# Q's result leaves a projection block through two half-row buffers and two stores, not through one buffer of the row pool

## The chip, the core and the metric

The kernel runs on one core of a Trainium2 chip. The metric is the device time of one launch in microseconds. Five engines work side by side, each on its own queue in order: TensorE (PE, with its weight loads shown as PEld), VectorE (DVE), ScalarE (ACT), GpSimd (POOL) and SyncE (SP). In this kernel DMAs are issued by SP and by POOL. An engine that meets an instruction whose input or buffer is not ready stands there with all that is queued behind it.

## What is computed

A transformer layer in float32 on x of shape (2, 2048, 1024), cut here to what matters:

```python
x = x + attn(layernorm(x))
x = x + ffn(layernorm(x))

def attn(x):                      # one head, D = 256
    q, k, v = split(x @ Wqkv + bqkv)
    a = softmax(q @ k.T / sqrt(256))
    return (a @ v) @ Wo + bo

def ffn(x):                       # HID 1024, INT 2048, LAT 512
    rw = sum of the top 2 of x @ gate_w
    shared = relu(x @ up_w) ** 2 @ down_w
    routed = ((x @ fc1_w) @ expert_w * rw) @ fc2_w
    return layernorm(shared + routed) * ln_gamma + ln_beta
```

## The kernel before, in words

Every float32 matrix product is made of three products of float32r parts (high times high, low times high, high times low), so each operand is split into a high and a low part first: ACT casts the high part, DVE subtracts it for the low one (`split`, L141).

**The stage around the change** is the projection of x to q, k and v, about the first 300 us. It runs over eight blocks of 512 rows, numbered here 0 to 7 by the order in which they run. For each block `qkv_block` (L427) does eight parts: four v tiles of 128 rows (`v_tile`, L437), then two chunks of q and two of k (`qk_chunk`, L461), of 512 columns each. Each part gathers its sum in a PSUM bank of the pool `psa`, which has four. DVE takes a v tile out of its bank (L456, L457) into half of a half-row tile; two v tiles share one such tile, which is split into high and low parts one part later. ACT takes q and k out of theirs (L472, L475). k and v of the first four blocks go to DRAM from their own pools (L486). q goes to DRAM for every block, since the attention stage reads it later: before the change both chunks are written to one tile of the row pool, `got["q"]`, and after the second chunk POOL issues one store of 512 KB, `q_d` (L481).

**Beside each part** a function `after` (L740) puts work for the next block into the order. After the v tiles j = 0 to 3 `NormBlock.step` (L306) normalises the next block's four rows of 128 x 1024. Two of the four have their moments taken by ACT (`Moments`, L255: L262 sums, L274 squares; each writes a throw-away tile `junk` from the half-row pool, L269), the two others by DVE (L179). ACT writes the normalised row (L286), DVE transposes 32 x 32 tiles of it into `xblk` (L214), POOL stores that (`xt_d`, L219) and fetches it back in another order (`xt`, L227). After the fourth v tile come the last `xt` fetch and, for blocks 0 to 5, the four loads of the rows of the block after next (`xrow`, L193 called from L762). After the second q chunk and the two k chunks the fetched tiles are split into the next block's operands (`xha`, `xla`, L143 and L144); the fourth is split after the next block's first v tile, ahead of the first moments.

**What sets the order.** Blocks 0 to 6 stand in a `manual_schedule` region: every engine's queue has the order of the program. Block 7 and the attention stage stand outside it and are ordered by a planner; the feed-forward stage is again in written order.

**The pools.** A tile gets its buffer when it is allocated in that order; when all buffers of the pool are taken, the first instruction that writes the new tile waits until the last user of an old one has ended, a DMA included. The row pool (L71) has nine buffers of 128 x 1024 float32 for the x rows, `xblk`, `xt` and, before the change, q. When q is allocated, four x rows and four `xt` tiles hold eight of the nine. The half-row pool (L72) has four buffers of 128 x 512 float32. In the projection stage it serves the bias of v (`bv`, L106, from the start to the last v tile), the v tiles (two tiles per block, one after the other) and `junk` (four per block).

Of the kernel before, what the change touches and what calls it, by code (L numbers as in the profile page):

```python
# [11 lines left out]
AF = mybir.ActivationFunctionType  # L12
# [7 lines left out]
W = 512  # L20
# [5 lines left out]
def kernel(  # L26
# [21 lines left out]
    nc = tc.nc  # L48
# [7 lines left out]
    NDC = D // P  # L56
# [30 lines left out]
    def row(name):  # L87
        return rp.tile([P, C], FP, tag="r", name=name)

    def half(name):  # L90
        return hp.tile([P, W], FP, tag="h", name=name)

    def bank(pool, name):
        return pool.tile([P, W], FP, tag="b", name=name)

    def f32(t):
        return t.bitcast(FP)
# [14 lines left out]
    q_d = [dram.tile([P, C], FP, name=f"q_d{i}") for i in range(NBLK)]  # L112
# [36 lines left out]
    def split_late(t, hi, lo):  # L149
        nc.scalar.copy(hi, t)  # L150
        late_ops.append(lambda: nc.vector.tensor_tensor(lo, t, f32(hi), ALU.subtract))  # L151

    def flush():
        for f in late_ops:
            f()
        late_ops.clear()
# [11 lines left out]
    def cols(w, i, n):  # L168

        return w.rearrange("(c p) i -> p c i", p=P)[:, :, ts(i, n)]  # L170
# [168 lines left out]
    def x_chunk(xT, c, sl=slice(0, W)):  # L339
        return tuple(v.rearrange("p (c n) -> p c n", n=W)[:, c % 4, sl] for v in xT[c // 4])  # L340

    def piece(pr, c, n, sl):
        return tuple(v.rearrange("p (c n) -> p c n", n=n)[:, c, sl] for v in pr)
# [79 lines left out]
    def hl(t):  # L423

        return t.rearrange("p (s n) -> p s n", s=2)

    def qkv_block(n, wqkv, xT, parts, after):  # L427

        keep = n < BPB
        units = {a: (unit if n == BPB - 1 else ex_unit)(f"{a}{n}") for a in "kv"}
        if keep:
            kv[n] = [units["k"], units["v"]]
        got = {}

        def v_tile(t):  # L437
            pm = bank(psa, "pv")
            if t % 2 == 0:
                got["v"] = half("v")  # L440

            for c in range(NCC):
                xh, xl = x_chunk(xT, c, ts(t, P))
                w = wqkv[2][c // 4].rearrange("p (c n) -> p c n", n=2 * D)[:, c % 4]
                ops = [(pm, xh, w), (pm[:, :D], xl, w[:, :D])]
                for i, (o, x_, w_) in enumerate(ops[:: -1 if c % 2 else 1]):
                    nc.tensor.matmul(  # L447
                        o,
                        lhsT=x_,
                        rhs=w_,  # L450
                        start=c + i == 0,
                        stop=c == NCC - 1 and i == 1,
                        skip_group_check=True,
                    )
            vt = got["v"][:, ts(t % 2, D)]
            nc.vector.tensor_tensor(vt, pm[:, :D], bv_sb, ALU.add)  # L456
            nc.vector.tensor_tensor(vt, pm[:, D : 2 * D], vt, ALU.add)  # L457
            flush()
            split_late(vt, *(hl(units["v"])[:, s, ts(t, D)] for s in range(2)))

        def qk_chunk(a, dc):  # L461
            i = "qk".index(a)
            pm = bank(psa, "pq")
            acc = Pass3(pm, NCC)
            for c in range(NCC):
                acc.add(piece(wqkv[i], c, D, ts(dc, P)), x_chunk(xT, c))
            bias = bqk_sb[:, i * NDC + dc : i * NDC + dc + 1]
            flush()
            if a == "q":
                if dc == 0:  # L470
                    got["q"] = row("q")
                nc.scalar.activation(got["q"][:, ts(dc, W)], pm, AF.Identity, bias=bias)  # L472
            else:
                h, l = (hl(units[a])[:, s, ts(dc, W)] for s in range(2))
                nc.scalar.activation(h, pm, AF.Identity, bias=bias)  # L475
                nc.vector.scalar_tensor_tensor(l, pm, bias, f32(h), ALU.add, ALU.subtract)

        for j, (a, i) in enumerate(parts):
            v_tile(i) if a == "v" else qk_chunk(a, i)
            if (a, i) == ("q", NDC - 1):  # L480
                nc.gpsimd.dma_start(out=q_d[n], in_=got["q"])  # L481
            after(j)
        flush()
        if not keep:
            for a, d in (("k", k_d), ("v", v_d)):
                nc.gpsimd.dma_start(out=d[n], in_=f32(units[a]))  # L486
# [247 lines left out]
    def a_block(i, norm, xT, x3):  # L734
# [5 lines left out]
        def after(j):  # L740
# [23 lines left out]
            elif j > NB:  # L764
                split_tile(norm.x[j - NB - 1], j - NB - 1, nxt[0])

        qkv_block(order[i], wqkv, xT, V + QK, after)
        if nxt:
            return (after_next or [None])[0], nxt[0], lambda: split_tile(norm.x[3], 3, nxt[0])

    wqkv, xT = {}, new_xT("a")
    with tc.manual_schedule():
# [3 lines left out]
        for i in range(NBLK - 1):  # L776
            norm, xT, x3 = a_block(i, norm, xT, x3)
            if i == 1:
                for h in range(C // W):
                    nc.gpsimd.dma_start(  # L780
                        out=cols(fc2e, h, W), in_=fold[h].rearrange("p (c n) -> p c n", n=W)
# [371 lines left out]
    with tc.manual_schedule():  # L1153
        for b in range(NBB):
# [73 lines left out]
            for m, (p, i) in enumerate(UPS[b]):  # L1228
# [63 lines left out]
                elif m >= 2 * NK and p != "p7":  # L1292
                    n = {"p4": "p6", "p6": "p5", "p5": "p3", "p3": "p7"}[p]
# [46 lines left out]
            for j, p in enumerate(("p1", "p2", "p6", "p5", "p3", "p7", "p4")):  # L1340
# [12 lines left out]
                for k in range(NK - late):  # L1353
# [4 lines left out]
                    if more:  # L1358
# [3 lines left out]
                        if j >= 5 and k % 2 and k < 2 * NB:  # L1362
                            n = "p1" if j == 5 else "p2"
# [18 lines left out]
                if late:  # L1382
                    last_w = [next_piece() for _ in range(late)]
                    both = unit("last")
                    while len(sp) < late:
                        i = len(sp) + len(sp_cast) - late + 2
# [78 lines left out]
```

## Time and profile before

| | |
|---|---|
| median of 3 runs | 2318.88 us (2317.77 to 2319.33) |
| the profiled execution's own time | 2317.74 us |
| its span, first to last instruction | 2315.8 us |
| granted TensorE clock | 0.999 |
| PE busy | 2301.2 us |
| ACT, L472, q out of PSUM | 16 instructions, 686 ns median |
| POOL, L481, q's store | 8 of 512 KB, 537 to 558 ns to issue, 3.3 to 10.5 us to landing |
| POOL, L193, loads of x rows | 24 of 512 KB, 540 ns median to issue |

The views of one profiled execution are shown. A line of a timeline has the start in us, the length in us, the engine, the line of the kernel, the operation, the tiles written and read, how many were merged, and in brackets how long the engine had stood idle before it and for whom. A line of the waits has the total wait, the number of waits and the longest. A line of the stretches has the length, the busy time of PE, PEld, DVE, ACT and POOL with the number of instructions, the granted clock, the share of the DMA engines that was busy, and GB/s. A line of DMA issues ends with the time from the issue to the landing.

### The profile page before, as it was taken

How to read it: one execution, taken by the hardware profiler on the slowest of the kernel's cores; microseconds unless marked ns; L12 is line 12 of the kernel's file. 1: busy time of each engine (PE TensorE's matmuls, PEld its weight loads, DVE VectorE, ACT ScalarE, POOL GpSimd, SP SyncE). 2: the span in 40 equal slices, each digit the busy share in tenths (PEclk: the TensorE clock that was granted, in tenths of full speed). 3: DMA queues.
4: the chain of work that ended last, by engine and by line, in shares of the span. 5: the costliest groups of instructions: out<-in, count | busy, mean ns of one | idle time of the engine just before them, and what ended most of it. 6: DMA issues, size and time to landing. Idle time of an engine off the chain costs nothing.

```text
span 2315.8 us, 28854 instructions
## 1 busy us (share of the span) xinstructions
PE 2301.2 (99%) x10332; PEld 1893.0 (82%) x10332; DVE 1567.1 (68%) x2458; ACT 1184.5 (51%) x1950; POOL 286.9 (12%) x434
## 2 busy tenths in 40 slices
PE   9999999999999999999999999999999999999998
PEld 7888888888888788888888888888888887888886
DVE  6666569888888575797665577765456667435656
ACT  6555455555544633766562474674045557214245
POOL 3222211011000111110110111110000011000000
PEclk9999999999999999999999999999999999999999
DMA  7878759899976677786787698686568579566684
GB/s 258 298 275 279 245 153 253 237 301 295 229 186 195 218 222 228 256 288 196 217 244 254 214 320 306 193 242 222 192 218 273 195 233 290 190 192 192 204 246 150
DMA packets 237023, 544.21 MB, mean 235 GB/s; under 512 B 18592, under 2 KB 105120, under 8 KB 234832
## 3 DMA queue, kind: packets, MB, share of 16 engines
q1 hardware_dynamic: 170448, 302.56, 39.6%
q0 software_dynamic: 66432, 239.81, 35.3%
q8 instruction: 82, 1.34, 0.2%
q14 instruction: 61, 0.50, 0.1%
HBM read 412.78 MB, written 180.37 MB: 256 GB/s over the span
## 4 chain that ended last, share of the span: by engine, by line
PE 89%; DVE 5%; DMA 2%; ACT 2%; issue 2%; POOL 0%; SPq 0%; DVEq 0%; ACTq 0%; POOLq 0%
PE pd L131 32%; PE pu L131 32%; PE ps L131 8%; PE po L131 8%; PE pw L131 4%; PE pq L131 3%; DVE xblk L214 1%; PE pg L990 1%; PE pv L447 1%; DMA xt_d<-xblk 1%; PE pf L131 1%; DVE xla L144 1%; DVE st L179 1%; DMA w<-wt_lead 0%; DVE v L457 0%
## 5 line engine op out<-in xcount | busy, mean ns | idle before, releaser
L131 PE MATMUL pd<-w,sp 128*128 128x512 f32 x3336 | 758.2, 389 | 0.6 <-DVE sp L1202 0.5
L131 PEld LDWEIGHTS pd<-w,sp 128*128 128x128 f32 x3336 | 625.9, 188 | 131.7 <-DVE sp L1202 1.9
L131 PE MATMUL pu<-xh,w 128*128 128x512 f32 x2240 | 690.6, 389 | 0.0
L131 PEld LDWEIGHTS pu<-xh,w 128*128 128x128 f32 x2240 | 420.4, 188 | 89.6 <-DVE w L941 0.5
L131 PE MATMUL pu<-xl,w 128*128 128x512 f32 x1120 | 436.0, 389 | 0.0
L131 PEld LDWEIGHTS pu<-xl,w 128*128 128x128 f32 x1120 | 210.3, 188 | 44.3 <-DVE xl L151 0.3
L1197 ACT CAST sp<-h 128x512 fp32r<-128x512 f32 x238 | 146.6, 618 | 155.9 <-PE pd L131 118.7
L934 ACT CAST w<-w 128x512 fp32r<-128x512 f32 x251 | 153.3, 616 | 138.6 <-DMA w<-wt 116.1
L941 DVE TENSOR_TENSOR w<-w 128x512 fp32r<-128x512 f32 x251 | 171.9, 687 | 75.4 <-ACT w L934 75.1
L1202 DVE TENSOR_TENSOR sp<-h,sp 128x512 fp32r<-128x512 f32 x238 | 163.1, 687 | 68.9 <-ACT sp L1197 68.7
L131 PE MATMUL po<-p,v 128*128 128x512 f32 x768 | 194.1, 391 | 0.0
L131 PE MATMUL ps<-q,k 128*128 128x512 f32 x768 | 192.5, 390 | 0.0
L131 PEld LDWEIGHTS ps<-q,k 128*128 128x128 f32 x768 | 143.7, 188 | 29.9 <-ACT max L630 0.2
L131 PEld LDWEIGHTS po<-p,v 128*128 128x128 f32 x768 | 143.2, 188 | 29.2
L1143 ACT ACTIVATE h<-h 128x1024 f32<-128x1024 f32 x48 | 50.8, 1057 | 220.4 <-DVE h L1260 158.5
L151 DVE TENSOR_TENSOR xl<-xt,xh 128x512 fp32r<-128x512 f32 x108 | 74.4, 689 | 128.1 <-ACT xh L150 125.6
L627 ACT COPY s<-ps 128x512 f32<-128x512 f32 x128 | 74.9, 586 | 142.0 <-PE ps L131 141.7
L214 DVE STREAM_TRANSPOSE xblk<-xrow 128x1024 f32<-128x1024 f32 x60 | 121.0, 2016 | 9.4 <-ACT xrow L286 9.2
L632 DVE TENSOR_TENSOR max<-ps,max 128x512 f32<-128x512 f32 x120 | 82.4, 686 | 33.2 <-ACT s L627 32.1
L944 POOL DMA_DIRECT2D w_p<-w x95 | 50.7, 534 | 405.8 <-DVE w L941 314.6
L131 PE MATMUL pq<-xha,w_h 128*128 128x512 f32 x256 | 99.8, 390 | 0.2 <-DVE v L457 0.2
L131 PE MATMUL pq<-xla,w_h 128*128 128x512 f32 x256 | 99.6, 389 | 0.0
(199 smaller groups left out, 2999.9 us busy)
## 6 DMA issues: line engine op xcount, KB each, us to landing
w<-w_p SPq DMA_DIRECT2D x230, 512.0 KB, 3.9
w<-wt SPq DMA_DIRECT2D x235, 256.0 KB, 3.4
w_p<-w POOLq DMA_DIRECT2D x95, 512.0 KB, 4.4
xt_d<-xblk POOLq DMA_DIRECT2D x56, 512.0 KB, 4.2
xt<-xt_d POOLq DMA_DIRECT2D x56, 512.0 KB, 5.8
xres<-in_L_attn_x_dram SPq DMA_DIRECT2D x32, 512.0 KB, 7.0
xres<-in_L_attn_bo_dram POOLq DMA_DIRECT2D x32, 512.0 KB, 10.3
x<-xres SPq DMA_DIRECT2D x32, 512.0 KB, 4.8
```

Of the source, the lines that this page charges most:

```text
L131: nc.tensor.matmul(self.ps, lhsT=a, rhs=b, start=self.i == 0, stop=self.i == self.n - 1, skip_group_check=self.on,)
L144: eng.tensor_tensor(lo, t, f32(hi), ALU.subtract)
L151: late_ops.append(lambda: nc.vector.tensor_tensor(lo, t, f32(hi), ALU.subtract))
L214: nc.vector.transpose(b.rearrange("p (q k i) -> p q k i", q=P // SQ, i=SQ), r.rearrange("p (k i q) -> p q k i", k=NCC, i=SQ),)
L627: nc.scalar.copy(s["s"][k // 4][:, ts(k % 4, W)], pm)
L632: nc.vector.tensor_tensor(s["max"], pm, s["max"], ALU.max)
L934: nc.scalar.copy(w[:, 0:W], raw)
L941: nc.vector.tensor_tensor(w[:, W : 2 * W], raw, f32(w)[:, 0:W], ALU.subtract)
L944: nc.gpsimd.dma_start(out=kept[key], in_=w.bitcast(FP))
L1143: nc.scalar.activation(o, v, AF.Relu)
L1197: nc.scalar.copy(t[:, 0:W], v)
L1202: add(t[:, W : 2 * W], v, f32(t)[:, 0:W], ALU.subtract)
```

## The change

Each chunk of q gets a half-row tile of its own and its own store of 256 KB, issued right after the chunk is taken out of PSUM. The row pool no longer serves q, and the single store after the second chunk is gone. The pools keep their sizes.

```diff
@@ in qk_chunk
             if a == "q":
-                if dc == 0:
-                    got["q"] = row("q")
-                nc.scalar.activation(got["q"][:, ts(dc, W)], pm, AF.Identity, bias=bias)
+                q = half("q")
+                nc.scalar.activation(q, pm, AF.Identity, bias=bias)
+                nc.gpsimd.dma_start(out=q_d[n][:, ts(dc, W)], in_=q)
             else:
@@ at the end of qkv_block
         for j, (a, i) in enumerate(parts):
             v_tile(i) if a == "v" else qk_chunk(a, i)
-            if (a, i) == ("q", NDC - 1):
-                nc.gpsimd.dma_start(out=q_d[n], in_=got["q"])
             after(j)
```

## The prediction

> **What bounds the kernel now.** I read the page's busy times first, then PE by stage, then who waits for whom between 64 and 270 us (blocks 1 to 6 of the projection stage), then the order of work on ACT, POOL, DVE and PE there, and last the transfers' times to landing.
>
> ```profile
> PE 2301.2 (99%) x10332; PEld 1893.0 (82%) x10332; DVE 1567.1 (68%) x2458; ACT 1184.5 (51%) x1950; POOL 286.9 (12%) x434
> ```
>
> TensorE leaves 14.6 us of a span of 2315.8 idle, so a change outside it can win at most that. In the stage that the change touches there is less: PE is busy for the whole of every stretch between 50 and 300 us but one.
>
> ```profile
> 180.00:220.00 40.00, 40.00 (x192) 33.34 (x191) 29.26 (x58) 23.98 (x43) 10.20 (x17) 1.00 0.76 265
> 220.00:260.00 40.00, 39.79 (x190) 32.91 (x190) 28.61 (x50) 22.80 (x40) 11.83 (x19) 1.00 0.84 281
> ```
>
> ```profile
> ACT q L472 <- DMA xt_d<-xblk: 41.1, 6, 7.0
> ...
> POOL xt L227 <- ACT q L472: 4.4, 1, 4.4
> ...
> PE pq L131 <- DVE v L457: 0.2, 1, 0.2
> ```
>
> The first line is the wait that the change aims at: in six blocks ACT stands before q's result for some 6.9 us, because q takes its buffer from the row pool and gets the one that the last transposed row still leaves through. The last line says what this costs PE today: 0.2 us.
>
> ACT around one block boundary (start, length, engine, line, operation):
>
> ```profile
> 97.19 1.27 ACT L472 ACTIVATE q<-pq,bqk_sb 128x512 f32<-128x512 f32 x2 [6.90 <-DMA xt_d<-xblk]
> ...
> 101.57 1.15 ACT L143 CAST xha<-xt 128x512 fp32r<-128x512 f32 x2
> 104.84 0.41 ACT L150 CAST v<-v 128x256 fp32r<-128x256 f32 x1 [2.12 <-DVE v L457]
> 105.15 1.14 ACT L143 CAST xha<-xt 128x512 fp32r<-128x512 f32 x2
> 106.19 1.05 ACT L262 ACTIVATE junk<-xrow 128x1024 bf16<-128x1024 f32 x1
> ```
>
> POOL before it, and how long its fourth row load and q's store took to land:
>
> ```profile
> 97.62 0.77 POOL L227 DMA_DIRECT2D xt<-xt_d  x1 [2.81 <-issue]
> 98.38 2.12 POOL L193 DMA_DIRECT2D xrow<-in_L_attn_x_dram  x4
> 100.49 0.54 POOL L481 DMA_DIRECT2D q_d<-q  x1
> ```
>
> ```profile
> xrow<-in_L_attn_x_dram POOLq DMA_DIRECT2D x1, 512.0 KB, 8.1
> q_d<-q POOLq DMA_DIRECT2D x1, 512.0 KB, 8.8
> ```
>
> q's store is queued behind four 512 KB loads: the fourth, issued at 99.97, lands at 108.1 and q's store at 109.3. The same store in the last block (290.58), with nothing ahead, lands after 3.3 us.
>
> DVE and PE after the boundary:
>
> ```profile
> 116.02 0.42 DVE L457 TENSOR_TENSOR v<-pv,v 128x256 f32<-128x256 f32 x1
> ```
>
> ```profile
> 249.68 0.47 PE L131 MATMUL pq<-xha,w_h 128*128 128x512 f32 x1 [0.21 <-DVE v L457]
> ```
>
> The second q chunk of a block uses the PSUM bank of that block's second v tile (pool psa has four), which L457 frees. It is freed 10.25 us after the block's first junk in each of blocks 1 to 6 (106.19 to 116.44), and the chunk starts soon after: 84.33, 117.23, 150.14, 183.16, 216.18 and 249.68, so the slack is 1.1, 0.8, 0.4, 0.15, 0.3 and 0. PE has almost no cover for a later junk.
>
> **The change, part by part.**
>
> *Removed: q's wait for a row buffer.* ACT can take q's first half at 89.9 in this block rather than at 97.19 (PE ended it at 84.3), and the second right behind. What is late next: the third split still waits for k's second chunk, which PE ends at 100.8, and the last two tiles' fetches (landed 99.4 and 101.8), and the v cast for PE's first v tile (103.4). So ACT would reach junk at about 105.8, not 106.19. PE can gain what it loses to this chain: its distances between blocks are 32.91, 32.90, 32.91, 33.14, 33.10 and 33.38, against 32.91 free, so 0.23 + 0.19 + 0.47 = 0.9 us over the stage.
>
> *Same work:* sixteen evictions of 0.69 us on ACT, none added. The row pool has one buffer more for x's rows; no row of the waits view but q's shows a wait for that pool, so nothing.
>
> *Added: eight DMA issues on POOL.* One of 0.54 us each, 4.3 us in all. They come behind the row loads; behind them are k_d, v_d and the weight sums of L409/L415, whose landing nobody in this stage waits for, and POOL is busy for 12% of the span. Nothing; without that cover 4.3 us. The later readers of q_d need both halves: the two at 265.1 read stores that landed by 242.3, and the load at 269.94 on SP (behind which stand the residual rows of the attention stage) reads block 6's, which then lands as one 512 KB store's worth as now. Nothing.
>
> *Added: a wait for a half-row buffer.* The pool `half` has four. One holds bv until the last v tile. Each block takes one for v tiles 0 and 1, four short ones for junk (L269), one for v tiles 2 and 3, and now two for q, held until q's stores land. When the next block begins, its first v pair takes the free one, bv and the two q halves hold the other three, and junk, allocated right after that v tile, finds none. It must take a q half and wait for its landing, as q did for xblk's. In the trace of before no junk waits, so the price comes from the landing rows.
>
> When does the first half land? POOL keeps the order of the program: xt, four loads, then q, whenever ACT was done (in block 6 q was ready at 257.8 and its store left at 264.51, behind the last xt at 263.76). So the half leaves at 100.49 in block 1, and at 67.11, 133.53, 168.37, 199.97 and 233.61 in the others. From there the fourth load lands after 8.6, 7.6, 8.4, 7.5, 8.9, 7.4 us (blocks 0 to 5; read from its row, less the 0.5 between the issues) and the whole q store after 9.9, 8.8, 9.6, 8.7, 10.5, 8.7. The first half carries half the bytes behind the same loads, so I take the middle: 9.2, 8.2, 9.0, 8.1, 9.7, 8.0, sum 52.2. Ends for the range: the fourth load (48.4), and the second half, which I put at the whole store plus 0.3 (58). Far below both lies the 3.3 of the lone store.
>
> junk stands 5.7 us behind the issue now (100.49 to 106.19). A landing after 8.2 makes it wait some 2.5. Queued behind it on ACT are the moments, the normalised rows, the v casts and q; DVE waits for those at L279 with the second v tile's eviction behind it; PE waits for that bank. And the delay adds up, since the chain closes on itself: from junk to the next q issue (normalise, transpose, xt_d, xt, four loads) the trace has 27.5, 27.3, 28.9, 27.2 and 28.0 us in blocks 1 to 5, with ACT and DVE nearly back to back and PE ahead of them. In block 3 the xt issue came 1.8 after its xt_d landed, not 0.5 (the 4.4 behind ACT q above); I drop that 1.3, leaving 137.6. Then the first junk of block 6 comes at 67.1 + 52.2 + 137.6 + six wake-ups of 0.1 (97.1 to 97.19 for q) = 257.5, against 239.28: 18.2 us late. One turn takes 27.5 + 8.7 + 0.1 = 36.3 where the blocks now follow each other in 33.3. In block 6 PE has no slack, so PE is 18.2 late there, and everything after runs at 99% PE and gives nothing back.
>
> The Trainium skill, "DMA: Bandwidth & Descriptors", section "Anatomy of one DMA — SWDGE (gpsimd) path", fits such a transfer as 2.0 us plus bytes over 436 GB/s: by estimate 2.6 us for a half and 3.2 for the whole, which the lone store's 3.3 agrees with and the 8.8 behind four loads does not. By that rule the half would land before junk is reached and the sum would be -0.9; by the rows it is +18.2, and I go by the rows, as the queue ahead is part of the landing. Its section "Bandwidth" asks for batches of 1 MiB and more, which speaks against halving a store.
>
> **Sum.** The profiled execution took 2317.74 (span 2315.8), so 2335.9; the median shown, 2318.88, is 1.1 above it: 2337.1. By the ends: 67.1 + 48.4 + 135.6 (0.4 less a turn for the xt lag) + 0.6 gives +12.4, 2331; 67.1 + 58 + 138.9 + 0.6 gives +25.3, 2344.
>
> **The rivals.**
> 1. *No junk waits* (ends on the other side). If a half lands within 5.7 us of its issue, the wait is gone and 0.9 us is won: 2318.0. The lone 3.3 speaks for it, the fourth load's 7.4 or more ahead in the same queue against it.
> 2. *The new v pair, not junk, gets a q half.* Then DVE's v eviction stands at the landing, and junk follows 2.3 later (103.93 to 106.19): 6 x 2.3 = 13.8 more, +32.0, 2351. Against it: the pair is allocated first, while one buffer is free.
> 3. *junk waits for the second half*: 2344, as above.
> 4. *The half lands in between*, at 6.5 us: 67.1 + 39 + 137.6 + 0.6 = 244.3, +5.0, 2324.
> 5. The last block and the attention stage are ordered by a planner, which may shift their order: some 2 us either way, inside the range.
>
> **How the numbers follow.** The main case 0.65, junk on the second half 0.10, the v pair 0.07, in between 0.06, no wait 0.12. The measurement tells 0.2%, 4.6 us. No wait is "same" but for 0.03 that something else wins more: faster 0.03, same 0.09, slower 0.88. The range 2323 to 2347 holds the main case, the second half and about half of "in between".
>
> **What would show it.** ACT q without a wait for xt_d; the four junk instructions (or v L456) of blocks 1 to 6 with waits for q_d of some 3 us each; PE idle of about 18 us at pq behind DVE v L457; the v tiles' starts 36 us apart; the stages after it unchanged but shifted. I am wrong if the half lands early, if POOL sends it ahead of the loads, or if a junk finds a free buffer.

## The result, and the profile after

The changed kernel takes 2329.72 us (median of 6 runs, 2328.98 to 2332.15) beside 2318.70 for the kernel before (6 runs, 2317.77 to 2320.36). The ratio is 1.0048, 95% interval 1.0038 to 1.0058: 11.0 us slower. The forecast was 18.2 us slower (2337.1), with a range of 2323 to 2347. The profiled execution of the changed kernel took 2329.25, its span 2327.4.

The page of the changed kernel, busy times:

```profile
PE 2304.1 (99%) x10332; PEld 1895.5 (81%) x10332; DVE 1568.1 (67%) x2458; ACT 1185.1 (51%) x1950; POOL 291.4 (13%) x442
```

The work is the same; PE's idle time went from 14.6 to 23.3 us, and its busy time from 2301.2 to 2304.1, 1.8 us of that in one chunk at a lower clock (last section). Who waits for whom between 60 and 310 us:

```profile
ACT junk L262 <- issue: 20.8, 6, 4.5
...
PE pq L131 <- DVE v L457: 8.4, 5, 2.4
```

The six waits of ACT before q (41.1 us) are gone. In their place stand six waits before the first `junk` of blocks 1 to 6, 20.8 us, and PE's wait for the second v tile's bank went from 0.2 to 8.4 us (the prediction's signs had some 18 there, and a wait before each of a block's four `junk`; only the first waits). The profile names no releaser for these waits ("issue"); the times do. ACT at the boundary that the prediction showed (block 1 to block 2), then POOL before it and the time to landing of the fourth load and of q's first half:

```profile
105.52 1.14 ACT L143 CAST xha<-xt 128x512 fp32r<-128x512 f32 x2
110.17 1.06 ACT L262 ACTIVATE junk<-xrow 128x1024 bf16<-128x1024 f32 x1 [3.51 <-issue]
...
111.46 0.28 ACT L183 ACTIVATE sd<-mv,eps 128x1 f32<-128x1 f32 x1
```

```profile
98.89 0.77 POOL L227 DMA_DIRECT2D xt<-xt_d  x1 [2.54 <-issue]
99.70 2.12 POOL L193 DMA_DIRECT2D xrow<-in_L_attn_x_dram  x4
101.82 1.09 POOL L472 DMA_DIRECT2D q_d<-q  x2
```

```profile
xrow<-in_L_attn_x_dram POOLq DMA_DIRECT2D x1, 512.0 KB, 8.1
q_d<-q POOLq DMA_DIRECT2D x1, 256.0 KB, 8.3
```

The first half leaves at 101.82, lands 8.3 us later at 110.1, and junk starts at 110.17. So it is in each of the six blocks (the store is that of the block before):

| block | first half issued | to landing | landed | junk in the changed kernel | junk before |
|---|---|---|---|---|---|
| 1 | 66.46 | 9.1 | 75.5 | 75.60 | 72.99 |
| 2 | 101.82 | 8.3 | 110.1 | 110.17 | 106.19 |
| 3 | 136.19 | 8.5 | 144.7 | 144.79 | 139.48 |
| 4 | 170.44 | 9.6 | 180.0 | 180.09 | 172.76 |
| 5 | 206.39 | 9.2 | 215.6 | 215.68 | 205.62 |
| 6 | 241.88 | 8.3 | 250.2 | 250.29 | 239.28 |

The delay of junk grows from 2.6 to 11.0 us. DVE and PE in block 2, where the second v tile's bank is freed and the second q chunk takes it:

```profile
118.89 0.42 DVE L457 TENSOR_TENSOR v<-pv,v 128x256 f32<-128x256 f32 x1
```

```profile
119.46 0.47 PE L131 MATMUL pq<-xha,w_h 128*128 128x512 f32 x1 [1.40 <-DVE v L457]
```

The second q chunk of block 6 starts at 259.60 and not at 249.68, 9.9 us late, and the stage's last chunk ends at 309.50 and not at 299.15, 10.3 us late. The span is 11.6 longer: what the stage lost stays lost, as the later stages keep PE full, and in the feed-forward stage of this execution PE waits 1.1 us more for DVE than in the one of before (1.6 and 0.5).

### The profile page after: what moved, and what is told of

Same layout as the page of the kernel before. It is cut to its first block, busy times and chain, and to the rows that moved or that the text cites. A ratio compares the mean times of both kernels' runs of the same rounds, so it can differ in the third digit from the quotient of the medians.

```text
span 2327.4 us, 28898 instructions
## 1 busy us (share of the span) xinstructions
PE 2304.1 (99%) x10332; PEld 1895.5 (81%) x10332; DVE 1568.1 (67%) x2458; ACT 1185.1 (51%) x1950; POOL 291.4 (13%) x442
## 4 chain that ended last, share of the span: by engine, by line
PE 86%; DMA 4%; DVE 3%; issue 3%; ACT 2%; POOL 1%; DVEq 0%; POOLq 0%; ACTq 0%; SPq 0%
PE pd L131 31%; PE pu L131 31%; PE ps L131 8%; PE po L131 7%; PE pw L131 4%; PE pq L131 2%; DVE xblk L214 1%; PE pg L988 1%; DMA q_d<-q 1%; PE pf L131 1%; DMA xt<-xt_d 1%; DMA xt_d<-xblk 1%; DMA w<-wt_lead 0%; ACT junk L274 0%; ACT junk L262 0%
## 5 line engine op out<-in xcount | busy, mean ns | idle before, releaser
L131 PE MATMUL pq<-xha,w_l 128*128 128x512 f32 x256 | 100.4, 392 | 0.0
```

The lines of the kernel that those rows point to most:

```text
L131: nc.tensor.matmul(self.ps, lhsT=a, rhs=b, start=self.i == 0, stop=self.i == self.n - 1, skip_group_check=self.on,)
```

## The experiments

All ratios are to runs of the kernel before on the same chip.

**1. junk without the half-row pool.** The moments' throw-away tile of the projection stage moves to the row pool, which has a buffer to spare since q left it.

```diff
         def junk(self):
-            return half("junk").bitcast(mybir.dt.bfloat16)
+            t = row("junk")[:, 0:W] if self.early else half("junk")
+            return t.bitcast(mybir.dt.bfloat16)
```

(Lines that pass `early` on are left out here; it is set by `NormBlock` alone.)

> The changed kernel, with the throw-away tile of the moments in the projection stage taken from the row pool, where a buffer is free since q left it, and not from the half-row pool. My theory (junk waits for a q half's landing, and that wait is the whole loss): ACT junk without a wait in blocks 1 to 6, PE idle before pq under 1 us, some 2318 us, 11 below the changed kernel and within 2 of the kernel before. Rival (the loss comes from the second store and the shorter rows themselves, or from the freed row buffer's new order): 2328 to 2331, as the changed kernel.

Measured: 2317.32 us, ratio 0.9995 (0.9986 to 1.0005). ACT and PE in this kernel:

```profile
104.23 1.14 ACT L143 CAST xha<-xt 128x512 fp32r<-128x512 f32 x2
105.27 1.05 ACT L262 ACTIVATE junk<-xrow 128x1024 bf16<-128x1024 f32 x1
```

```profile
220.00:260.00 40.00, 40.00 (x193) 33.61 (x192) 27.39 (x50) 22.57 (x40) 12.40 (x20) 1.00 0.83 281
```

junk starts with no wait, and PE waits for nothing in blocks 1 to 6. The q stores are as before the edit, two of 256 KB behind four loads, and land after 8.2 to 9.5 us; only nobody waits for them. So the whole loss hangs on junk's buffer. Run again in more rounds, with the question whether the two buffers win anything once junk does not wait:

> The kernel of junk_in_rows once more, in more rounds, to see whether the two half-row buffers win anything where junk does not wait. My working has 0.9 us to win (PE's distances between blocks back to 32.91), a ratio of 0.9996; the rival that q's wait cost more than PE's idle shows would give 0.998 or less. Where the interval spans 1, the trace alone tells of the 0.9.

Measured: 2318.30 us, ratio 0.9993 (0.9984 to 1.0002). The time does not tell it from the kernel before. In the first of its two profiles the blocks follow each other at 32.9 us throughout, and from the first q chunk to the end of the last k chunk the stage takes 252.3 us (45.34 to 297.62; 252.3 in the second profile too) beside 253.2 in the one profile of the kernel before (45.97 to 299.15): the 0.9 us of the prediction, and no more.

**2. The row loads behind q's stores.** The four loads are issued after the second q chunk, so that in POOL's queue the two halves stand ahead of them.

```diff
             if j == NB - 1:
                 norm.step(NB)
-                if i + 2 < NBLK:
-                    after_next.append(NormBlock(load_block(xf, order[i + 2], nc.gpsimd)))
                 nxt.append(new_xT(f"a{i}"))
             elif j > NB:
+                if j == NB + 1 and i + 2 < NBLK:
+                    after_next.append(NormBlock(load_block(xf, order[i + 2], nc.gpsimd)))
```

> The changed kernel, with the four row loads issued after the second q chunk and not after the fourth v tile, so that on POOL the two q stores stand ahead of them, still behind the last xt fetch. My theory (the four loads ahead in the queue make the landing late): a q half lands some 4 to 5 us after its issue, 1 to 2 us before junk is reached, no junk wait, some 2318 us. Rival (POOL's position does not matter, the bytes of the stage do): landing after 8 us or more, 2326 to 2330 us.

Measured: 2320.40 us, ratio 1.0003 (0.9994 to 1.0012). The times to landing of the q stores between 60 and 245 us, first in the changed kernel, then in this one:

```profile
DMA to landing us min/median/max: 8.3/8.8/9.7
```

```profile
DMA to landing us min/median/max: 4.6/4.8/5.8
```

The same stores land in 4.8 us rather than 8.8 when the loads stand behind them. junk then waits 2.0 us in all of the stage, none of it for q's store, and the loss is gone. In this kernel the landing is late because of what stands ahead in POOL's queue, and that is the written order.

**3. q's stores on SP.**

```diff
-                nc.gpsimd.dma_start(out=q_d[n][:, ts(dc, W)], in_=q)
+                nc.sync.dma_start(out=q_d[n][:, ts(dc, W)], in_=q)
```

> The changed kernel, with the sixteen q stores issued on SP and not on POOL, so that they do not stand behind the four row loads. My theory (the landing is late because of the queue ahead of it): a q half lands within 4 us of its issue and long before junk, junk without a wait, some 2318 us. Rival (a half-row store lands late in this stage whatever queue it is on, since the 16 DMA engines are full of the same bytes): landing after 6 to 8 us, but as the issue is some 8 us earlier the junk wait would still shrink to nothing or 1 us; then the two theories differ in the landing alone.

Measured: 2322.15 us, ratio 1.0011 (1.0002 to 1.0020). On this queue nothing stands ahead, and still the halves land after 5.3 to 7.5 us, not within my 4; the rival's 6 to 8 was nearer. But they leave some 9 us (block 0) to 16 us (block 5) earlier than in the changed kernel. junk waits once, for 1.2 us before 207.08, and not for q, which had landed at 197.72, but by the times for its x row (landed at 207.01). Most of the loss is gone. Some 2.6 us remain: PE stands for 1.4 us before second q chunks, and for 2.4 in block 7's v tiles, for splits of the fetched tiles. The q stores go at the time when the transposed tiles are stored and fetched back, and what waits longer in this kernel (between 100 and 310 us) is the split for its fetched tile and DVE's statistics for their row:

```profile
ACT xha L143 <- DMA xt<-xt_d: 18.7, 9, 8.0
...
DVE st L179 <- DMA xrow<-in_L_attn_x_dram: 5.1, 4, 1.7
```

In the kernel before, the first of these is 6.5 us in the same stretch and the second does not occur; the second is 4.0 us in experiment 2 as well, which loses nothing by it. That the stores took the other transfers' share of the DMA engines fits this, but was not tried by itself.

**4. Eight PSUM banks.** The parts of a block go over all eight banks, so that no q chunk needs a v tile's bank of its own block.

```diff
-            pm = bank(psa, "pv")
+            pm = bank((psa, psb, psc, psa)[t], "pv")
...
-            pm = bank(psa, "pq")
+            pm = bank(((psa, psb), (psc, psa))[i][dc], "pq")
```

> The changed kernel, with the v tiles and the q and k chunks spread over all eight PSUM banks (pools psa, psb and psc) and not over psa's four, so that a chunk of q no longer needs the bank of a v tile of its own block. My theory (the wait closes a chain on itself, junk to junk through the transposes, the fetch, the loads and the q store, and takes some 35 us per turn where PE needs 32.9): the junk waits stay, and PE is caught later, by the splits of the next block; 2 to 5 us won of the 11, some 2325 to 2328. Rival (PE only ever loses at the bank, block by block): 2318 to 2320.

Measured: 2332.30 us, ratio 1.0055 (1.0040 to 1.0070); the changed kernel's interval overlaps it. Nothing was won, so both expectations missed the number, the rival by far. Waits of the stage in this kernel:

```profile
ACT junk L262 <- DMA q_d<-q: 25.4, 4, 7.3
...
ACT junk L262 <- issue: 7.4, 2, 5.1
```

```profile
PE pv L447 <- ACT xha L143: 7.3, 6, 4.6
...
PE pv L447 <- DVE xla L144: 2.0, 7, 0.5
```

The profile names q's store as what junk waits for in four of the six blocks here. PE runs ahead through the free banks and is then caught by the splits of the next block, as my theory has it. What I put at 2 to 5 us did not come: the longest gap, 4.6 us, now comes in block 7, and the clock is at half when PE resumes. In these lines PE's busy time is the second number, and the granted clock stands behind the five engines (1.00, then 0.55, 0.50, 0.50):

```profile
280.00:282.00 2.00, 0.00 (x0) 0.00 (x0) 0.00 (x0) 0.00 (x0) 2.00 (x5) 1.00 0.90 348
282.00:284.00 2.00, 0.00 (x0) 0.00 (x0) 1.26 (x3) 1.91 (x4) 0.23 (x1) 0.55 1.06 363
284.00:286.00 2.00, 1.45 (x4) 0.94 (x5) 2.00 (x5) 0.84 (x2) 0.00 (x0) 0.50 0.98 354
286.00:288.00 2.00, 2.00 (x7) 1.69 (x7) 1.46 (x5) 0.41 (x1) 0.00 (x0) 0.50 1.03 418
```

By the trace some 3 us go to the clock: block 7's v tiles take 20.2 us, against 11.3 in the kernel before, and 5.9 of that are waits. Another 2.2 us are the chain, which is no shorter here but longer (junk of block 6 starts at 253.35, 3.1 later than in the changed kernel, in an execution that began 0.9 later). Why block 7's gap is so long, and what part the planner's order has in it, is left open.

**5. A fifth load ahead of the stores.**

```diff
                     after_next.append(NormBlock(load_block(xf, order[i + 2], nc.gpsimd)))
+                    load_row(xf[ds(order[i + 2] * W, P), :], nc.gpsimd)
```

> The changed kernel with a fifth row load of 512 KB (into a row buffer that nobody reads) behind the four, so ahead of q's stores, in blocks 0 to 5. My theory (junk waits for the first q half, and the wait is paid anew in each turn of the chain junk to q store to junk): the first half lands about 1.3 us later in each of six turns (0.5 of it for POOL's issue), junk comes six times 1.3 later, some 8 us on top: 2336 to 2340. Rival (the loss of each block is its own, with no chain): the same 1.3 once, 2330 to 2332.

Measured: 2339.78 us, ratio 1.0087 (1.0070 to 1.0104), 21.1 us above the kernel before, 10 more than the changed kernel. junk of block 6 starts at 260.64, 10.4 us later than in the changed kernel; 0.9 of that is the execution's later start (first q chunk at 46.30 and 45.41), so each of the six turns grew by 1.6. Paid once it would have been 1.6. In this execution (2342.40 us, the longest of the four) another 2.5 us are a chunk of block 6 at a lower clock (last section). The waits of the stage:

```profile
ACT junk L262 <- issue: 15.2, 3, 6.8
...
ACT junk L262 <- DMA q_d<-q: 13.8, 3, 5.4
```

**6. Half-row buffers in blocks 0 to 2 alone.**

```diff
             if a == "q":
-                q = half("q")
-                nc.scalar.activation(q, pm, AF.Identity, bias=bias)
-                nc.gpsimd.dma_start(out=q_d[n][:, ts(dc, W)], in_=q)
+                if order.index(n) < 3:
+                    q = half("q")
+                    nc.scalar.activation(q, pm, AF.Identity, bias=bias)
+                    nc.gpsimd.dma_start(out=q_d[n][:, ts(dc, W)], in_=q)
+                else:
+                    if dc == 0:
+                        got["q"] = row("q")
+                    nc.scalar.activation(got["q"][:, ts(dc, W)], pm, AF.Identity, bias=bias)
+                    if dc == NDC - 1:
+                        nc.gpsimd.dma_start(out=q_d[n], in_=got["q"])
```

> Q's two half-row tiles and stores in blocks 0 to 2 alone; blocks 3 to 7 as before the change (row buffer, one store). My theory: junk waits in blocks 1 to 3, is 5.3 us late in block 3 as in the changed kernel, and nothing after gives it back, since PE is full: before + 5, some 2324. Rival (the later blocks have slack and take the delay in): 2319 to 2321.

Measured: 2323.23 us, ratio 1.0018 (1.0009 to 1.0028), 4.5 us. junk is late by 6.5 us in block 3 (145.98) and, with no q half to wait for any more, still by 6.0 in block 6 (245.25); 0.4 of both is the execution's later start. The later blocks give back at most 0.5: the delay is kept.

**7. Two stores from one row buffer.** The kernel before, with each half of q's row buffer stored right after its eviction.

```diff
-                nc.scalar.activation(got["q"][:, ts(dc, W)], pm, AF.Identity, bias=bias)
+                q = got["q"][:, ts(dc, W)]
+                nc.scalar.activation(q, pm, AF.Identity, bias=bias)
+                nc.gpsimd.dma_start(out=q_d[n][:, ts(dc, W)], in_=q)
...
-            if (a, i) == ("q", NDC - 1):
-                nc.gpsimd.dma_start(out=q_d[n], in_=got["q"])
```

> The kernel before with the stores alone changed: q stays in one row buffer, but each half of it is stored by its own DMA, right after its eviction. My theory (a second store and shorter rows cost nothing by themselves): ACT q still waits 6.9 us for xt_d in six blocks, no junk waits, 2317 to 2320. Rival (the second store, its issue on POOL or its 2 KB rows cost time): 2321 or more.

Measured: 2317.53 us, ratio 0.9996 (0.9986 to 1.0005). The wait that the change removes is all there, and neither it nor the second store with its 2 KB rows adds anything that the time shows; the interval leaves room for 1.2 us. (The stage takes 254.6 us in this one profile, 253.2 in that of before.)

```profile
ACT q L473 <- DMA xt_d<-xblk: 42.7, 6, 7.8
```

## Why the prediction was right, and where its size was off

- **q's wait for a row buffer was worth 0.9 us.** Shown: experiment 7 keeps the wait and takes the time of before, experiment 1 has neither wait and wins 0.9 us by its traces. The times alone do not tell so little.
- **The issues on POOL cost nothing.** Shown by experiment 7 (eight issues more, and no loss over its interval's 1.2 us, where they would be 4.3 without cover). Nor does halving the store, which the prediction held against the change.
- **junk must wait for a q half.** Shown: the table's landings and starts agree within 0.1 us in six blocks, and experiment 1 takes the loss away by giving junk another buffer. It is the first half that it waits for: the second half of block 1's q lands at 110.7, after junk of block 2 has begun at 110.17. Rivals 1 to 4 fall with this and with landings after 8.3 us and more; the v pair stands where it did, its adds ending at 105.18 (104.8 before).
- **The landing behind four loads.** I had 52.2 us for the six landings, and 53.0 were measured, each 0.3 to 0.8 after the fourth load's. Experiment 2 shows that the loads ahead make it late (4.8 us without them). The 2.6 us that the prediction worked out from the Trainium skill ("DMA: Bandwidth & Descriptors", section "Anatomy of one DMA — SWDGE (gpsimd) path") leave the queue out; where nothing stands ahead, in block 7, a half lands after 2.2 to 2.3 us.
- **The chain that closes on itself.** Shown by experiment 5 (10 us more for 1.6 us more per turn), by experiment 6 (a delay that stays), and by the growth in the table: from junk to junk the turns take 34.9 us on average, where 36.3 were forecast and PE by itself needs 32.91. Experiment 4 shows that the bank is only where PE meets it.
- **The term that was mis-sized: the turn from junk to the next q issue.** I took its five values of before, 137.6 us; measured are 26.2, 26.0, 25.7, 26.3 and 26.2, in all 130.4. This is all of the error in junk's time (257.5 forecast, 250.3 measured; the first issue came 0.6 earlier, the landings 0.8 later). The step that failed is "ACT and DVE nearly back to back": in each turn of before ACT waited 1.0 us, after the first sum, for DVE's statistics of the second row. DVE makes these without junk, so while ACT stands before junk they get done, and the wait behind it is gone. The wait in the kernel before (block 2, then all six blocks), and DVE in the changed kernel:

```profile
108.56 0.29 ACT L183 ACTIVATE sd<-mv,eps 128x1 f32<-128x1 f32 x1 [0.99 <-DVE mv L181]
```

```profile
ACT sd L183 <- DVE mv L181: 6.0, 6, 1.0
```

```profile
107.38 1.28 DVE L179 BATCH_NORM_STATS2 st<-xrow 128x6 f32<-128x512 f32 x2
108.69 0.21 DVE L181 BATCH_NORM_AGGREGATE mv<-st 128x2 f32<-128x12 f32 x1
```

The statistics end at 108.9, before junk starts at 110.17, and `sd` at 111.46 follows with no wait, where the same line waited 0.99 us in the kernel before (108.56, after a junk at 106.19). From the first junk to the second it is 1.5 us and not 2.6, and from junk to the freed bank 9.15 and not 10.25. Five turns by 1.1 are 5.5 of the 7.2. Most of the other 1.7 lies in the turns of blocks 3 and 5, which in the trace of before were longer than the rest (27.6 after my correction, and 28.0) and are not so here; there the last transposed row landed 4.8 us after its issue, and 3.9 and 4.4 now. No run was made for this alone, but experiment 6 holds both cases in one execution. In its blocks 1 to 3 junk waits and `sd` does not; in blocks 4 to 6 it is the other way round, and from the first junk to the second it is 1.5 us and then 2.6. The turns take 26.4, 26.3 and 26.7 us, then 27.8 and 27.7:

```profile
147.27 0.28 ACT L183 ACTIVATE sd<-mv,eps 128x1 f32<-128x1 f32 x1
...
180.72 0.29 ACT L183 ACTIVATE sd<-mv,eps 128x1 f32<-128x1 f32 x1 [0.99 <-DVE mv L181]
```

The same 1.1 us is gone once more on the last way, from block 6's junk to the bank. So the forecast's own sum, with the turns as measured, puts junk 18.2 less 7.2, that is 11.0 us late, and PE 9.9 us late, which is what the traces show. That the launch is 11.0 us longer as well, and not 9.9, is in part chance: 0.4 us was added in the rest of the stage, and the remainder stands outside it. The main case, the direction and the range held.

## What to carry to other kernels

A wait for a buffer that is moved from one pool to another is not removed until the new pool is counted at its fullest moment: here four buffers, of which bv, a v pair and two q halves left none for a tile that nobody reads. What a buffer is held for is the landing of its last transfer, and that depends on what stands ahead in the same queue: 8.8 us behind four loads, 4.8 before them (and 5.3 to 7.5 on another queue with nothing ahead, at a time when other transfers ran). When a new wait lies in a chain that repeats, work out the length of one turn against the period of the bounding engine, and take out of the turn every wait that the new one covers.

## What was not expected of the hardware

TensorE's granted clock fell after short gaps. In block 5 of the changed kernel PE stands 2.40 us before its second q chunk (224.97), and soon after the clock is at half:

```profile
222.96:226.38 3.42, 1.41 (x6) 1.22 (x7) 3.28 (x10) 2.94 (x5) 0.33 (x1) 1.00 0.37 153
226.38:229.79 3.41, 3.41 (x9) 2.65 (x9) 3.34 (x7) 1.72 (x3) 1.32 (x2) 0.50 0.31 126
```

The chunk takes 7.2 us rather than 5.4. It cost nothing there, since block 6's bank was freed only at 259.45, just as PE came to it. With the fifth load the same happened behind gaps of 2.6 and 2.7 us in blocks 1 and 3 and of 4.7 in block 6, where the chunk took 7.9 us and lay on the path; a gap of 3.3 us in block 5 of that kernel was followed by a chunk of 5.6 us at full clock. So it is not the length of the gap alone that decides. The Trainium skill, "TensorE: Matmul & The Clock Gate", section "Part 1: The HAM clock gate (the "warmup" mystery)", has the clock halved after at least one idle window of some 3.4 us that runs freely. The halved clock agrees; the gaps of 2.4 to 2.7 us are shorter than that window.

The traces show more. The half clock lasts 3.41 us here (226.38 to 229.79) and after the gaps of 2.6 and 2.7, and 6.83 in block 6 with the fifth load, where the stretches of full clock in between are 20 and 31 times 3.413 us long: the clock changes on a grid of 3.41 us, and that much of the page's rule is seen. But a stretch of that grid need not be idle throughout. The gap of 3.3 us that cost no clock fell into two stretches, with 1.49 and 2.02 us of matmuls:

```profile
227.26:230.67 3.41, 1.49 (x7) 0.92 (x5) 3.15 (x3) 3.31 (x8) 0.56 (x1) 1.00 0.67 267
230.67:234.09 3.42, 2.02 (x9) 1.70 (x10) 3.28 (x9) 2.65 (x4) 0.00 (x0) 1.00 0.40 161
```

The fall in block 5 of the changed kernel came after a stretch with 1.41 us of matmuls (above), the other falls in the projection stage (three with the fifth load, one with eight banks) after stretches with 0.45 to 1.33. So in these runs 2.0 us without matmuls in one such stretch halved the clock in the next, and 1.9 did not. This is read off the traces, with PE's busy time as the profile models it; no run was made for it.
